# Snake convolutions: where the first three chunks of hats lie, and the order of the last 9x9 sums against the second chunk's hats

## The chip, the cores and the metric

One core of one Trainium2 chip runs the whole program. The metric is device time in microseconds, as a median of several runs; one further execution was profiled. In the profile, TensorE is PE (with PEld for its weight loads), VectorE is DVE, ScalarE is ACT, GpSimd is POOL, and SyncE is SP. SP does no arithmetic here: it issues the transfers (DMAs), one after the other in program order.

## The reference, cut to what matters

The program is four layers on an image x of 2 x 128 x 64 x 64: an attention layer, a snake-convolution layer (L1), three steps of two 3x3 convolutions, and a four-direction selective scan. The change is in L1, which computes

```python
h  = gelu(affine(conv2d(x, cv1_w, 1), cv1_g, cv1_b))             # 64 channels
o0 = silu(affine(conv2d(h, conv0_w, K // 2), conv0_g, conv0_b))  # 9x9
ox = dsconv(h, ..., morph=0)   # nine samples along a row, shifted by learnt offsets
oy = dsconv(h, ..., morph=1)   # the same along a column
out = silu(affine(conv2d(concatenate([o0, ox, oy]), fuse_w, 0), fuse_g, fuse_b))
```

In dsconv, a 3x3 convolution of h gives offsets, whose running sums from the centre tap give a position for each pixel and tap; h is sampled there with linear interpolation, the samples are multiplied with the weights w, and the result is group-normalised. Then the layer gates out and adds x.

## The kernel before, in words

`layer1` (L466 on) first calls `stem_and_wide`, then `snakes`. `stem_and_wide` computes the stem (h, kept as `hz`) and the 9x9. The 9x9 is done with a fast scheme: six combinations of the columns of h, `comb[0]` to `comb[5]`, are multiplied on TensorE with six transformed weights (`w`, L590), in the order x = 1, 2, 3, 4, 0, 5, once for each half k of the image. After each x, VectorE and ScalarE gather the products into the four sums s, p, d and q of each image b; a sum that is complete gets its silu on ScalarE (L658) and is put on the list `ready`. `fuse` (L598) multiplies a ready sum with its part of the fuse weights, and copies the product into the image `xa`, on VectorE for image 0 (L604) and on ScalarE for image 1 (L602). The jobs that x leaves on the list are fused after the products of the next x; so the two s of x = 0 are fused behind the products of x = 5, and the two q of x = 5 last.

The snakes sample by multiplication with hats. For each chunk of 4 lines (17 chunks for each of two directions, called chunk 0, 1, 2 and so on here), `positions` has SP load 1 MB of positions from the scratch `pos` in DRAM, broadcast to the partitions, by four transfers of 256 KB each (L794). `hat` turns them into interpolation weights in place: an absolute value on ScalarE (L802), then a subtraction and a minimum on VectorE (L803). `transposed` puts lines of h on the partitions (L784, copied by ScalarE in L785); `sample` multiplies lines with hats into PSUM (L859), copied to `feat` by ScalarE for image 0 (L873) and VectorE for image 1 (L871); `convolve` multiplies the samples with the weights of the taps (L885 and L896), once for every two chunks from the third on.

Class `Ahead` does some of this beside the last products of the 9x9 (second half, x = 0 and x = 5). `load` fetches the offset and tap weights; `convs` computes the offsets ahead of the products of x = 5; `beside` is called before each pair of those products: at n = 2 it writes the positions to `pos` and loads chunks 0 and 1 (`positions(0, m, near[m])`), at n = 12 and 15 it transposes lines, and at n = 24 it makes the hats of chunk 0. What it fills lies in the tile `early`, of pool l1big, which outlives the 9x9: `early` is a window of four combinations, `comb[1]` to `comb[4]`, whose space is filled anew once their products are done. `comb[0]` and `comb[5]` lie in the pool of the 9x9, l1a.

`snakes` opens its pools where l1a was. Chunks go round four slots: `near[0]` and `near[1]` in `early`, and `hats0` and `hats1`, allocated in `snakes`. So chunks 2 and 3 are loaded into space that the 9x9 has used until its end. The body of `snakes` first issues the load of chunk 2 and the hats of chunk 1 (`positions(0, 2)`, `hat(0, 1)`). Step n then loads chunk n + 3, transposes lines for n + 2, samples chunk n, makes the hats of chunk n + 2, and at even n from 2 on convolves.

[...] The build does not always keep the written order there: the hats of chunk 1, written in `snakes`, stand some places earlier. So the order is given as built. ScalarE's order at the end of the 9x9 is: L802 of chunk 0, L802 of chunk 1, L602 (s of image 1), L658 twice (q), L602 (q of image 1). VectorE's is: L803 of chunk 0, L803 of chunk 1, L604 (s of image 0), L655 twice (the adds that complete q), L604 (q of image 0).

Of the kernel before, what the change touches and what calls it, by code (L numbers as in the profile page):

```python
# [10 lines left out]
F32 = mybir.dt.float32  # L11
# [9 lines left out]
P = 128  # L21
NB = 2
HW = 64
# [7 lines left out]
KC = K9 // 2  # L31
# [434 lines left out]
def layer1(g, I):  # L466

    nc, tc = g.nc, g.tc
    with ExitStack() as ctx:
        big = ctx.enter_context(tc.tile_pool(name="l1big", bufs=1))
        hz = big.tile([P, H8, H8], F32, name="hz")
        fw = big.tile([P, 3, P], F32, name="fw")
        nc.scalar.dma_start(fw, I["fuseT"])
        early = big.tile([P, 4, 3, HW // 2 + KC, HW // 4], F32, name="early")
        dr = ctx.enter_context(tc.tile_pool(name="l1dr", bufs=1, space=bass.MemoryType.DRAM))  # L480
        pos = dr.tile([64, L], F32, name="pos")
        ahead = Ahead(g, I, hz, early, pos)
        stem_and_wide(g, I, hz, fw, early, ahead)
        with ExitStack() as bctx:
            snakes(g, bctx, hz, ahead, fw)


def stem_and_wide(g, I, hz, fw, early, ahead):
# [10 lines left out]
    NF = HW // 4  # L499
# [3 lines left out]
    with ExitStack() as ctx:  # L503
# [1 line left out]
        ps = ctx.enter_context(tc.tile_pool(name="l1ps", bufs=8, space=PSUM))  # L505

        spdq = [[a.tile([P, BLK], F32, name=f"{n}{b}") for n in "spdq"] for b in range(NB)]
        comb = [early[:, i - 1] if 0 < i < 5 else a.tile([P, NQ, CR, NF], F32, name=f"comb{i}") for i in range(NX)]

        cw = comb[5].rearrange("p q r i -> p (q r i)")[:, : 9 * 64].rearrange("p (t o) -> p t o", o=64)  # L510
        nc.sync.dma_start(cw, I["cv1T"])
# [83 lines left out]
        def fuse(k, b, c, t):  # L595

            pf = ps.tile([P, BLK], F32, name="m")
            nc.tensor.matmul(pf, fw[:, 0, :], t, start=True, stop=True)  # L598
            xv = interior(g, b, k * RP, RP)[:, :, c : c + 4 * NF - 3 : 4]
            src = pf.rearrange("p (r i) -> p r i", i=NF)  # L600
            if b:
                nc.scalar.copy(xv, src)  # L602
            else:
                nc.vector.tensor_copy(xv, src)  # L604

        with tc.manual_schedule():
            for k in range(NBLK):
                stem(k)
                if k < 3:
                    wide_weights(0, 3 * k)  # L610
                if k * RB < CR:
                    combine(0, 1, k * RB, min((k + 1) * RB, CR))
            for t0 in (3, 0, 6):
                wide_weights(1, t0)
            for x in (3, 0, 5):
                combine(0, x, 0, CR)
            ready = []
            for k in range(HW // RP):
                for x in (1, 2, 3, 4, 0, 5):
                    last = k == HW // RP - 1  # L620
                    if last and x == 0:
                        ahead.load(w)
                    if last and x == 5:
                        ahead.convs(ps)
                    m = [ps.tile([P, BLK], F32, name="m") for b in range(NB)]
                    for n, pair in enumerate(zip(*(product(m[b], x, b, k) for b in range(NB)))):
                        if last and x == 5:
                            ahead.beside(n, ps)
                        for f in pair:
                            f()  # L630
                    for job in ready:
                        fuse(*job)
                    ready = []
                    for b in range(NB):
                        s, p, d, q = spdq[b]
                        if x == 1:
                            nc.scalar.copy(s, m[b])
                        elif x == 3:
                            nc.scalar.copy(p, m[b])
                        elif x == 2:  # L640
                            nc.vector.tensor_sub(d, s, m[b])
                            nc.vector.tensor_add(s, s, m[b])
                        elif x == 4:
                            nc.vector.tensor_sub(q, p, m[b])
                            nc.vector.tensor_add(p, p, m[b])
                            stt(d, q, 2.0, d, ALU.mult, ALU.add)
                            stt(q, q, 6.0, d, ALU.mult, ALU.add)
                            nc.vector.tensor_add(s, s, p)
                            stt(p, p, 3.0, s, ALU.mult, ALU.add)
                            ready += [(k, b, 1, d), (k, b, 2, p)]  # L650
                        elif x == 0:
                            nc.vector.tensor_add(s, s, m[b])
                            ready.append((k, b, 0, s))
                        else:
                            nc.vector.tensor_add(q, q, m[b])  # L655
                            ready.append((k, b, 3, q))
                    for _, _, _, t in ready:
                        nc.scalar.activation(t, t, AF.Silu, bias=vec(g, "conv0_b"), scale=vec(g, "conv0_g"))  # L658
                    if k == 0 and x not in (1, 3):
                        combine(1, {2: 1, 4: 3}.get(x, x), HW - CR, HW)  # L660
            for job in ready:
                fuse(*job)


class Ahead:
# [6 lines left out]
    def __init__(self, g, I, hz, early, pos):  # L672

        self.g, self.I, self.hz, self.pos = g, I, hz, pos
        e = early.rearrange("p n q r i -> p (n q r i)")
        self.at = 0

        def take(n):
            self.at += n
            return e[:, self.at - n : self.at]  # L680

        self.dsc = take(2 * P).rearrange("p (d o) -> p d o", d=2)
        self.dsw = take(2 * KC * P).rearrange("p (d t o) -> p d t o", d=2, t=KC)
        self.grp = take(P)
        self.lines = take(self.SLOTS * self.CN * 64).rearrange("p (r i c) -> p r i c", r=self.SLOTS, i=self.CN)
        self.near = [self.as_hats(take(2 * self.NT * self.CN * HW)) for _ in range(2)]
        self.cmat = take(64)
        self.ov = take(3)
        self.ob = take(1)
        self.placed = None  # L690

    def as_hats(self, t):
# [2 lines left out]
    def load(self, w):  # L695

        g, I = self.g, self.I
        dma = g.nc.sync.dma_start
        c = w.rearrange("p y q x o -> p (y q) (x o)")[:, :, P : 5 * P]
        self.yt = c[:64, 0:NBLK]  # L700
        self.grid = c[:, 8:12]
        self.th = [c[:, 12], c[:, 13]]
        self.y0 = [c[:, 14], c[:, 15]]
        self.ow = [c[:, 16 + t // 8, t % 8 * 64 : t % 8 * 64 + 64] for t in range(9)]
        dma(c[:, 16].rearrange("p (t o) -> p t o", o=64), I["offT"][:, :8])
        dma(self.ow[8], I["offT"][:, 8])
        for e in range(2):
            half = slice(64 * e, 64 * e + 64)
            dma(self.ov[half], I["offv"])
            dma(self.cmat[half], I["cum"])  # L710
            dma(self.grid[half], I["grid"].rearrange("p (k e x) -> p k e x", e=2, x=BLK)[:, :, e, :])
        g.nc.vector.scalar_tensor_tensor(
            self.ob, self.ov[:, 0:1], self.ov[:, 1:2], self.ov[:, 2:3], ALU.mult, ALU.add
        )
        dma(self.grp, I["grp_div"])
        for b in range(2):
            half = slice(64 * b, 64 * b + 64)
            dma(self.dsc[half], I["dscT"][:, :, KC])
            dma(self.dsw[half], I["dscT"][:, :, b * (KC + 1) : b * (KC + 1) + KC])
# [41 lines left out]
    def beside(self, n, ps):  # L761

        if n == 2:
            self.place(*self.placed, ps)
            for di in range(2):
                rows = slice(32 * di, 32 * di + 32)
                self.g.nc.sync.dma_start(self.pos[rows].rearrange("p (c x) -> p c x", c=NBLK), self.yt[rows])
            for m in range(2):
                self.positions(0, m, self.near[m])
        elif n in (12, 15):  # L770
            self.transposed(0, (n - 12) // 3, ps.tile([P, BLK], F32, name="m"))
        elif n == 24:
            self.hat(self.near[0])
# [32 lines left out]
def snakes(g, ctx, hz, ahead, fw):  # L806
# [10 lines left out]
    psf = ctx.enter_context(tc.tile_pool(name="l1psf", bufs=4, space=PSUM))  # L817
    psa = ctx.enter_context(tc.tile_pool(name="l1psa", bufs=1, space=PSUM))

    far = [ahead.as_hats(bp.tile([P, 2 * NT * CN * HW], F32, name=f"hats{i}")) for i in range(2)]  # L820
    slots = ahead.near + far
    feat = bp.tile([P, NB, RING, NT, HW], F32, name="feat")
    oraw = bp.tile([P, NB, L], F32, name="oraw")
    hats = {}
# [8 lines left out]
    def positions(di, m):  # L833

        if di < 2:
            hats[di, m] = slots[(di * NCH + m) % len(slots)]
            ahead.positions(di, m, hats[di, m])
# [118 lines left out]
        return turns  # L956

    with tc.manual_schedule():
        for m in range(2):
            hats[0, m] = slots[m]  # L960
        positions(0, 2)
        hat(0, 1)
        for n in range(2 * NCH):
            di, m = divmod(n, NCH)
            if m == 0:
# [1054 lines left out]
```

## Time and profile before

| what | value |
|---|---|
| median of 3 runs | 5577.32 us (5575.88 to 5578.47) |
| the profiled execution | 5576.86 us, of which its span is 5574.9 us |
| busy share of the span: PE, DVE, ACT, POOL | 85%, 81%, 73%, 65% |
| 9x9 products (L590), first to last start | 1147.6 to 1466.2 us |
| snake samples from the hats of slots hats0 and hats1 (L859), first to last start | 1494.3 to 1741.4 us |
| load of positions, four per chunk (L794) | 136 transfers of 256 KB, median 9.8 us from issue to landing |

Times in the trace are microseconds from the start of the span. The profiled execution took 1.96 us more than its span (work around the first and last instruction), and is 0.46 us below the median; so a difference read in the span is carried to the median as it is. The row of a stretch gives the busy time of each engine in it, and PEclk, the TensorE clock that was granted, as a share of the full clock. In the chain, each line is a piece of the work that ended last, with what it is and on which engine; SPq is the issue of a transfer, and DMA is the time from the end of the issue to the landing.

### The profile page before, as it was taken

To read this page: it belongs to the slowest core of one execution; us is meant where nothing else is said; L and a number is where in the kernel's file an instruction comes from. 1 tells how busy PE (TensorE), PEld (TensorE's weight loads), DVE (VectorE), ACT (ScalarE), POOL (GpSimd) and SP (SyncE) were. 2 spreads that over 40 slices of the span, in tenths; PEclk is the share of its full clock that TensorE was granted. 3 is DMA by queue.
4 is the path that set the end of the run, shared out by engine and by line. 5 is a ranking of instruction groups with operands and counts; after the bars stand their busy time and mean duration, and the time that the engine had idled before them with its cause. 6 is when DMAs were issued, how large, how long until landed. Compare 5 with 4: busy or idle time off the path is not lost.

```text
span 5574.9 us, 54509 instructions
## 1 busy us (share of the span) xinstructions
PE 4717.5 (85%) x17062; PEld 1756.9 (32%) x17062; DVE 4540.1 (81%) x4240; ACT 4087.5 (73%) x6282; POOL 3642.2 (65%) x1189
## 2 busy tenths in 40 slices
PE   6999999899887799878888777777787888777886
PEld 3444444344443344222222222222222222222221
DVE  6565655562245997799999999999999999999998
ACT  3999999600255212798888888888888888888886
POOL 6222222100000311699999999999999999999999
PEclk8999999999999999888887888888888887888887
DMA  4111111300464000555556555655655565565554
GB/s 155 39 46 41 36 31 38 62 1 16 79 122 78 22 0 0 125 129 142 134 127 142 138 132 127 145 127 136 151 129 130 139 142 133 128 142 136 136 134 106
DMA packets 335161, 554.27 MB, mean 99 GB/s; under 512 B 69408, under 2 KB 116016, under 8 KB 334736
## 3 DMA queue, kind: packets, MB, share of 16 engines
q1 hardware_dynamic: 333456, 549.27, 41.7%
q8 instruction: 135, 2.21, 0.2%
q10 hardware_dynamic: 1408, 1.46, 0.1%
q14 instruction: 162, 1.33, 0.1%
HBM read 461.40 MB, written 89.13 MB: 99 GB/s over the span
## 4 chain that ended last, share of the span: by engine, by line
DVE 43%; PE 35%; ACT 10%; issue 6%; DMA 2%; POOL 2%; SPq 1%; DVEq 0%; POOLq 0%; ACTq 0%
DVE db L1607 29%; DVE db L1571 10%; PE ps L312 8%; PE acc L328 8%; PE m L1161 6%; PE m L590 4%; ACT da L1593 4%; PE acd L896 2%; ACT db L1599 1%; DVE gt L1634 1%; PE m L550 1%; ACT L1458 1%; ACT u L1458 1%; PE pf L859 1%; POOL db L1617 1%
## 5 line engine op out<-in xcount | busy, mean ns | idle before, releaser
L1617 POOL TENSOR_TENSOR db<-db,c 128x2048 f32<-128x2048 f32 x512 | 2312.7, 4532 | 47.4 <-ACT hl L1612 33.0
L1593 ACT ACTIVATE da<-dd,am 128x512 f32<-128x512 f32 x2048 | 1398.3, 687 | 300.3 <-DVE db L1607 279.7
L1607 DVE TENSOR_TENSOR_SCAN db<-da,db 128x512 f32<-128x512 f32 x1376 | 1584.9, 1203 | 35.2 <-ACT db L1599 28.2
L318 ACT ACTIVATE e<-ps 128x1536 f16<-128x1536 f32 (+1 forms) x683 | 919.0, 1624 | 8.0 <-PE ps L312 8.0
L1607 DVE TENSOR_TENSOR_SCAN db<-da,hl,db 128x512 f32<-128x512 f32 x672 | 825.8, 1271 | 40.8 <-POOL db L1580 3.4
L1571 DVE TENSOR_TENSOR db<-pbc,dd 128x2048 f32<-128x2048 f32 (+1 forms) x384 | 780.7, 2033 | 31.5 <-PE pbc L1550 31.5
L1580 POOL TENSOR_TENSOR db<-b,dd 128x2048 f32<-128x2048 f32 (+1 forms) x192 | 772.7, 4025 | 13.8 <-DMA b<-bx 13.8
L1625 PE MATMUL py<-db,fold 128*32 128x512 f32 x4096 | 602.7, 674 | 153.9 <-POOL db L1617 153.7
L312 PE MATMUL ps<-q 128*128 128x512 f16 x2048 | 554.0, 379 | 4.3 <-DVE flag L260 2.7
L328 PE MATMUL acc<-e,v 128*128 128x512 f16 x2048 | 553.6, 379 | 0.1
L346 POOL TENSOR_TENSOR parts<-parts 32x512 f32<-32x512 f32 x64 | 80.5, 1257 | 707.8 <-DVE parts L345 707.8
L1599 ACT ACTIVATE db<-da,db,hl 128x1 f32<-128x1 f32 x1120 | 393.9, 352 | 148.7 <-DVE db L1571 103.6
L1212 POOL MEMSET v<- 128x256 f32 x2 | 1.1, 554 | 711.9 <-DVE b L1050 711.9
L339 DVE RECIPROCAL rec<-acc 32x512 f32<-32x512 f32 x64 | 214.9, 3358 | 257.8 <-PE acc L328 248.3
L1161 PE MATMUL m<-v,u 128*128 128x512 f32 x864 | 378.0, 600 | 43.1 <-DVE v L1104 41.5
L1518 PE MATMUL pm<-dd,ident 128*128 128x512 f32 x512 | 357.4, 836 | 2.9 <-ACT dd L1511 2.7
L1477 PE MATMUL pm<-u,wxp 128*72 128x512 f32 x256 | 186.4, 870 | 141.4 <-ACT u L1458 141.4
L1550 PE MATMUL pbc<-bc,sel 64*128 64x512 f32 x384 | 207.1, 539 | 109.2 <-DVE db L1571 108.4
L312 PEld LDWEIGHTS <-q 128*128 128x128 f16 x2048 | 197.7, 97 | 278.4 <-issue 103.8
L328 PEld LDWEIGHTS <-v 128*128 128x128 bf16 x2048 | 199.2, 97 | 248.9 <-issue 10.2
L1625 PEld LDWEIGHTS py<-db,fold 128*32 128x32 f32 x4096 | 90.0, 113 | 551.5 <-issue 326.0
L1453 PE MATMUL pm<-xn,wcs 128*128 128x512 f32 x512 | 235.3, 603 | 17.0 <-ACT xa L1652 10.5
(332 smaller groups left out, 6614.6 us busy)
## 6 DMA issues: line engine op xcount, KB each, us to landing
dd<-dx SPq DMA_DIRECT2D x1024, 256.0 KB, 6.4
dx<-dd SPq DMA_DIRECT2D x128, 512.0 KB, 5.5
c<-bx SPq DMA_DIRECT2D x1024, 64.0 KB, 2.1
b<-bx SPq DMA_DIRECT2D x512, 64.0 KB, 4.6
early<-pos SPq DMA_DIRECT2D x72, 256.0 KB, 9.8
piece<-qd SPq DMA_DIRECT2D x128, 128.0 KB, 2.8
hats<-pos SPq DMA_DIRECT2D x64, 256.0 KB, 9.7
piece<-kd SPq DMA_DIRECT2D x112, 128.0 KB, 2.7
```

What stands on the lines that cost most here:

```text
L312: nc.tensor.matmul(ps[:, i, :], t[:, 1, kb * P : (kb + 1) * P], t[:, 0, qb * BLK : (qb + 1) * BLK], start=True, stop=True,)
L318: nc.scalar.activation(e[:, :n, :], ps[:, :n, :], AF.Exp, scale=1.0 / UP**2)
L328: nc.tensor.matmul(acc, v3[b][:, kb, h, :], e[:, i, :], start=(kb == 0), stop=(kb == NS - 1))
L1161: nc.tensor.matmul(m[x], weights[j][:, dy, x, :], v[j][b][:, x, r0 : r0 + RP, :].rearrange("p r i -> p (r i)"), start=(dy == 0), stop=(dy ...
L1518: nc.tensor.matmul(ps, g.ident, S[i]["dd", hf][:, x, :], start=(x == 0), stop=(x == 1))
L1571: nc.vector.tensor_tensor(db_tile(k)[:, :, :n], G[k].pop("pb")[:, :n].unsqueeze(1).to_broadcast([P, 4, n]), S[i]["d4", hf][:, 1, :, :n], A ...
L1580: nc.gpsimd.tensor_tensor(db_tile(k)[:, :, n:], S[i]["b", ng][:, n:].unsqueeze(1).to_broadcast([P, 4, BLK - n]), S[i]["d4", hf][:, 1, :, n ...
L1593: nc.scalar.activation(da, S[i]["d4", hf][:, 0, q, :], AF.Exp, scale=am[:, hf, q, ng : ng + 1])
L1599: nc.scalar.activation(b0, da[:, first : first + 1], AF.Identity, bias=b0, scale=hl[:, hf, ng, q, :])
L1607: nc.vector.tensor_tensor_scan(d1, d0, d1, 0.0 if zero else hl[:, hf, ng, q, :], ALU.mult, ALU.add)
L1617: nc.gpsimd.tensor_mul(v, v, S[i]["c", ng].unsqueeze(1).to_broadcast([P, 4, BLK]))
L1625: nc.tensor.matmul(S[i]["y", hf][32 * q : 32 * q + 32, :], fold, G[k]["db"][:, q, :], start=False, stop=(ng == NNG - 1),)
```

## The change

`early` becomes a window of five combinations, `comb[0]` to `comb[4]`, and only `comb[5]` stays in l1a. The larger window holds three chunks of hats, `near[0]` to `near[2]`, now at its start, followed by the tap weights and the lines; three small constants (`cmat`, `ov`, `ob`) move to an unused corner of the 9x9's weights. `beside` loads three chunks at n = 2 instead of two, and `snakes` allocates one slot, `hats3`, instead of two. After the products of the last x = 5, the two s are not fused first: q is completed and gets its silu, then all four sums are fused. `hat` of chunk 1 is called at the end of `stem_and_wide` and no longer in `snakes`.

```diff
-        early = big.tile([P, 4, 3, HW // 2 + KC, HW // 4], F32, name="early")
+        early = big.tile([P, 5, 3, HW // 2 + KC, HW // 4], F32, name="early")
...
-        comb = [early[:, i - 1] if 0 < i < 5 else a.tile([P, NQ, CR, NF], F32, name=f"comb{i}") for i in range(NX)]
+        comb = [early[:, i] for i in range(5)] + [a.tile([P, NQ, CR, NF], F32, name="comb5")]
...
-                    for job in ready:
-                        fuse(*job)
-                    ready = []
+                    ended = last and x == 5
+                    if not ended:
+                        for job in ready:
+                            fuse(*job)
+                        ready = []
...
-                    for _, _, _, t in ready:
+                    for _, _, _, t in ready[2 * ended :]:
                         nc.scalar.activation(t, t, AF.Silu, bias=vec(g, "conv0_b"), scale=vec(g, "conv0_g"))
...
             for job in ready:
                 fuse(*job)
+            ahead.hat(ahead.near[1])
...
+        self.near = [self.as_hats(take(2 * self.NT * self.CN * HW)) for _ in range(3)]
         self.dsc = take(2 * P).rearrange("p (d o) -> p d o", d=2)
...
-        self.near = [self.as_hats(take(2 * self.NT * self.CN * HW)) for _ in range(2)]
-        self.cmat = take(64)
-        self.ov = take(3)
-        self.ob = take(1)
...
+        self.cmat, self.ov, self.ob = c[:, 17, 64:128], c[:, 17, 128:131], c[:, 17, 131:132]
...
-            for m in range(2):
+            for m in range(3):
                 self.positions(0, m, self.near[m])
...
-    far = [ahead.as_hats(bp.tile([P, 2 * NT * CN * HW], F32, name=f"hats{i}")) for i in range(2)]
-    slots = ahead.near + far
+    slots = ahead.near + [ahead.as_hats(bp.tile([P, 2 * NT * CN * HW], F32, name="hats3"))]
...
-        for m in range(2):
+        for m in range(3):
             hats[0, m] = slots[m]
-        positions(0, 2)
-        hat(0, 1)
```

In the built program the number of instructions of each engine and their order elsewhere are the same as before. ScalarE's order at the end of the 9x9 becomes: absolute value of chunk 0, silu of q twice, the two copies, absolute value of chunk 1. VectorE's becomes: minimum of chunk 0, the two adds of q, the two copies, the first two copies of samples, minimum of chunk 1.

## The prediction

> **What bounds the kernel now.** I read the page first: PE 85%, DVE 81%, ACT 73% of the span, which says nothing of one stage. The change lies around 1450 to 1500 us, so I asked for stretches there.
>
> ```profile
> core 0: us, PE busy (x) PEld busy (x) DVE busy (x) ACT busy (x) POOL busy (x), PEclk, DMA share, GB/s
> 1466.00:1468.60 2.60, 2.60 (x8) 0.68 (x4) 0.78 (x1) 0.02 (x1) 0.00 (x0) 1.00 0.21 50
> 1468.60:1474.20 5.60, 0.01 (x1) 0.00 (x0) 3.31 (x4) 3.80 (x4) 0.00 (x0) 0.94 0.00 0
> 1474.20:1479.10 4.90, 3.78 (x4) 1.18 (x4) 1.07 (x1) 1.74 (x2) 0.00 (x0) 0.50 0.00 0
> 1479.10:1486.30 7.20, 7.12 (x112) 6.49 (x112) 1.11 (x4) 1.37 (x6) 0.00 (x0) 0.68 0.77 90
> 1486.30:1494.30 8.00, 0.00 (x0) 0.00 (x0) 1.26 (x2) 3.23 (x4) 0.00 (x0) 0.77 0.86 179
> 1494.30:1501.10 6.80, 6.56 (x38) 3.41 (x38) 1.88 (x3) 2.75 (x4) 0.00 (x0) 0.77 0.79 154
> 1501.10:1598.00 96.90, 96.85 (x804) 55.89 (x808) 42.77 (x56) 52.43 (x66) 0.00 (x0) 1.00 0.80 148
> ```
>
> PE is without a gap in the 9x9 and again from 1501.1 to 1598. Between them it stands still twice (5.6 and 8.0 us), no bytes move for 10 us, and it works at a half clock after each halt. The chain of waits names the cause:
>
> ```profile
> 1459.24 9.23 DMA early<-pos
> ...
> 1468.58 2.01 ACT early L802
> ...
> 1470.61 1.23 DVE early L803
> 1471.84 0.97 DVE xa L604
> 1472.81 0.53 DVE q L655
> ...
> 1473.36 0.82 ACT q L658
> ...
> 1474.23 3.80 PE m L598 x4
> ...
> 1478.04 0.57 SPq L794
> ...
> 1487.15 11.10 DMA hats<-pos
> ...
> 1498.35 2.00 ACT hats L802
> ```
>
> So the last sums of the 9x9 stand in ACT's and DVE's queues behind the hats of chunk 1, whose positions land at 1468.5; only when those sums are fused (1478.0) may SP load chunks 2 and 3 into their space; and the landing of chunk 3 (1498.25) sets when PE goes on. SP's own wait has one line:
>
> ```profile
> SPq L794 <- PE m L598: 16.3, 1, 16.3
> ```
>
> **The order at the end of the 9x9.** After the change, ACT and DVE do the hats of chunk 0 first, as now: DVE ends them at 1465.55 + 1.23 = 1466.78. The products of x = 5 end at 1466.6. Then come the adds of q, 2 x 0.67 us, from 1466.8 to 1468.1 (they start at 1472.65 now). Now 1.58 us pass from the first add's start to PE's fuse (1472.65 to 1474.23), so q can be fused from 1468.4; the two s occupy PE from 1466.63 to 1468.61 and hide that. The fuse of q follows at once: 1.98 us as that of s took at full clock, in place of 3.80 at half. It ends at 1470.6, not 1478.0. ACT's last copy (L602, 1.06 us) ends at 1471.7, and PE starts the snakes at 1471.8, not 1479.16: 7.35 us earlier. Chunk 1's absolute value comes only after that copy (1471.7 to 1473.7), its minimum on DVE behind two small copies of samples (0.42 us) to about 1475.5. Queued behind it are the copies of chunk 0's samples, and PE's samples of chunk 1; before those PE has two transposes and the samples of chunk 0 to do (four microseconds at full clock), until 1475.9. So that moved piece costs nothing; if PE were faster, at most 0.5 us.
>
> **The load of chunk 2, moved.** Four transfers of SP go right behind chunk 1's eighth, from 1461.6 (1450.07 + 11.56), where SP has nothing to do until 1478. Nothing else is in SP's queue behind them but chunk 3's load. Their space, combinations 2 and 3, has been read for the last time when x = 3 ends; chunk 0 now lies on combination 0, whose products end at 1402, chunk 1 on combinations 1 and 2. No wait for the 9x9 is left on any of them.
>
> When does it land? ACT's first touch of each chunk shows the landings, since it waited for the DMA: 1463.52 (chunk 0), 1468.58 (1), 1491.01 (2), 1498.35 (3), 1506.03 (4), 1513.34 (5). With further chunks queued behind, one takes (1513.34 - 1491.01) / 3 = 7.44 us; with nothing behind, chunk 1 took 5.06. So chunk 2 lands between 1473.6 (5.06 behind chunk 1) and 1478.4 (1463.5 + 2 x 7.44); I take 1478, near the full queue, since the queue is now full. The earlier load may also slow chunk 1 to at most 1463.5 + 7.4 = 1470.9, which is before ACT reads it (1471.7).
>
> **The load of chunk 3.** Its slot lies where q of image 1 was, so it waits for the last fuse, 1470.6 instead of the present 1478.0 (SP issued it at 1480.6, behind chunk 2). Its landing from both sides: 1468.58 + 2 x 5.06 = 1478.7 at the fastest spacing; 1463.5 + 3 x 7.44 = 1485.8 at the full queue's. A third way: chunk 2 took 13.0 us from its first issue to ACT (1478.04 to 1491.01), which gives 1483.6. I take 1484.5, between the last two, nearer the row that the queue will be like. That is 13.85 us before 1498.35.
>
> **When PE goes on.** Now PE resumes the convolution at 1501.15, which is 2.80 us after ACT starts on chunk 3: ACT does the absolute value (2.00), a copy, and then the copies of chunk 2's samples, for which PE waits. After: 1484.5 + 2.8 = 1487.3. The other condition is PE's own work after chunk 2: absolute value 2.0, minimum 1.2, samples about 2.2, the first products of the convolution 2.1 + 1.1, with gaps some 9 us: 1478 + 9 = 1487. Both meet at 1487.3. Even with earlier landings PE can't be there before about 1484.4 (1475.5 for chunk 1's hats, then its samples, ACT's copies of them, and chunk 2's hats and samples).
>
> **The clock.** The Trainium skill, "TensorE: Matmul & The Clock Gate", Part 1, says that the clock halves after a wholly idle window of about 3.4 us, windows running freely, and comes back after as long a busy one. The row first: 5.6 and 8.0 us idle both led to 0.50, and the four matmuls behind the first took 3.8 us for 2.0. After the change one gap is left, from chunk 1's samples (1479) to chunk 2's hats (about 1481.5), 2.5 to 3 us. By the rule it is too short, and the sum stands. By the trace alone, which has no gap of that length at full clock, it could count as those did; then samples and first products (5.3 us) take twice as long, and the saving falls to about 9 us. The gap lies close to the limit that the rule gives, so this speaks against the change; I take the rule, since no idle window of its length fits in.
>
> **The rest costs nothing.** The three small constants move, and `load` makes the same eleven transfers; they are issued by 1387, and the constants are first needed when the running sums of the first offsets start at 1421.4. Chunk 4 may be issued once chunk 0 is sampled (1475) and SP has issued chunk 3 (about 1475), so the stream stays full. From then on PE binds (96.85 of 96.9 us) and everything is shifted, the two later layers too; nothing there runs to a time of its own.
>
> Sum: 1501.15 - 1487.3 = 13.9 us. The span goes from 5574.9 to 5561.0, the profiled time from 5576.86 to 5563.0; that execution was 0.46 below the median, so the median goes from 5577.3 to 5563.4.
>
> **The rivals.**
>
> - *The transfers are the bound.* If the stream keeps 7.44 us a chunk from chunk 0 on, chunk 5 is there at 1463.5 + 5 x 7.44 = 1500.7, 12.6 us earlier than 1513.34, and chunk 7 at 1515.6 against 1527.79, 12.2 earlier. PE has little cover (ACT waited for chunks 4, 5 and 7), so the saving shrinks to 12, or to 10 if the added transfers also delay chunk 0, for whose hats DVE's adds of q must wait: 5565.3 to 5567.3. For it: the DMA share of 0.8 throughout. Against it: 181 GB/s and more in single stretches.
> - *The clock halves in the new gap:* 9 us saved, 5568.3.
> - *Chunk 2 isn't early in effect* (some wait keeps it back until the last fuse at 1470.6): then only the order gains, 7.35 us, 5570.0.
> - *Chunks land at the fastest spacing:* PE's own limit, 1501.15 - 1484.4 = 16.7 us, 5560.6.
> - *Slower.* PE's granted clock falls in the stretch from 1487 to 1584, which is 96.9 us at full clock with PE never idle. At a mean clock f it costs 96.9 x (1/f - 1): the gain of 13.9 is gone at f = 0.875, and below f = 0.794 (25.1 us) the kernel is slower by over 0.2%; at 0.75 it costs 32.3, which gives 5577.3 + 18.4 = 5595.7. For it: the mean over the whole span is 0.883. Against it: 1.00 in this and in every stretch of the 9x9 without idle time, so the low values come with idleness.
>
> **How the numbers follow.** The forecast has 0.62, the slow transfers 0.20, the half clock 0.06, only the order 0.05, the fastest spacing 0.03, slower 0.04. The predicted time is 5563.4. Its own bounds, chunk 3 at 1485.8 or PE's limit, give 12.3 to 16.7 us: 5560.6 to 5565.0. For 8 in 10 I add the slow transfers, up to 5567.5, and a little below for a faster tail: 5559.5 to 5568.0. A measurement tells 0.2% from no change, 11.2 us, so 5566.2: faster holds the forecast, the fastest and two thirds of the slow transfers, 0.78; same holds the rest of these, the half clock and the order, 0.18; slower 0.04.
>
> **What the profile after would show.** The fuse of q (L598) ends near 1470.6 with four matmuls in 2 us; the snakes' first transpose near 1471.8; SP issues twelve transfers from 1450 in one run; ACT starts on chunk 2 near 1478 and on chunk 3 near 1484.5; PE runs without a gap from about 1487; PEclk stays 1.00. Wrong would be: ACT on chunk 3 past 1486, PE waiting for hats after 1490, PEclk 0.50 between 1475 and 1490, or chunk 0's hats later than 1463.5.

## The result, and the profile after

The changed kernel takes 5567.54 us (median of 21 runs, 5565.31 to 5571.33) against 5576.42 us before in as many runs: the ratio is 0.9985, with a 95% interval of 0.9978 to 0.9991. Two further comparisons gave 0.9985 (0.9977 to 0.9992) and 0.9984 (0.9976 to 0.9992). The kernel is faster by some 9 us, where 13.9 us were forecast; the time lies near the upper end of the range, and the change is a little under the 0.2% that were given as the bound of "faster".

The stretches of the profile after, cut at the same events as the stretches of before (the columns are those named in the prediction):

```profile
1468.50:1472.20 3.70, 3.65 (x10) 1.32 (x8) 3.22 (x5) 2.49 (x4) 0.00 (x0) 1.00 0.83 146
1472.20:1479.60 7.40, 6.13 (x112) 5.79 (x112) 2.36 (x6) 3.99 (x7) 0.00 (x0) 1.00 0.84 149
1479.60:1483.20 3.60, 0.01 (x1) 0.03 (x1) 1.32 (x2) 3.24 (x4) 0.00 (x0) 0.85 0.69 151
1483.20:1490.00 6.80, 6.80 (x37) 3.56 (x38) 1.10 (x2) 1.60 (x1) 0.00 (x0) 0.58 0.77 144
1490.00:1491.20 1.20, 0.61 (x3) 0.00 (x1) 0.77 (x1) 1.20 (x4) 0.00 (x0) 1.00 0.53 99
1491.20:1588.00 96.80, 96.80 (x810) 55.54 (x811) 43.79 (x56) 53.08 (x67) 0.00 (x0) 1.00 0.80 147
```

The halt of 5.6 us at the end of the 9x9 and the stretch without any transfer are gone. Of the two halts one is left, 3.6 us ahead of the samples of chunk 2, and the clock halves behind it (0.58 in that stretch). The products of the 9x9 end at 1468.5 here and at 1466.6 before, so times are compared from there. ACT's own timeline shows chunks 1 to 4:

```profile
1473.05 2.00 ACT L803 ACTIVATE early<-early,vecs 128x2048 f32<-128x2048 f32 x1
1479.84 2.00 ACT L803 ACTIVATE early<-early,vecs 128x2048 f32<-128x2048 f32 x1 [3.58 <-issue]
1488.40 2.00 ACT L803 ACTIVATE hats<-hats,vecs 128x2048 f32<-128x2048 f32 x1 [5.32 <-DMA hats<-pos]
1495.04 2.00 ACT L803 ACTIVATE early<-early,vecs 128x2048 f32<-128x2048 f32 x1 [3.41 <-issue]
```

Chunk 2 is there 11.3 us after the end of the products (24.3 before), chunk 3 after 19.9 us (31.7 before), and ACT, with nothing else ahead of it, waits 5.32 us for its landing (the positions of chunk 3 lie in `hats`). The chain of waits runs accordingly:

```profile
1468.52 3.65 PE m L598 x8
...
1472.19 1.07 ACT xa L602
...
1473.30 1.04 PE pb L785 x13
...
1483.36 7.31 DMA early<-pos
1490.67 0.49 ACT feat L873
...
1491.20 6.28 PE acd L896 x14
```

The eight matmuls of the last fuse are one run of 3.65 us at full clock, as forecast; behind them come the start of the snakes, up to 1479.6, and then nothing but transfers before the convolution's resumption at 1491.20. The chain names a load into `early` there, chunk 4's; that it is chunk 3's landing that counts is read from ACT's own row above, since the copy L873 that PE waits for stands in ACT's queue behind the absolute value of chunk 3.

Three profiles of each kernel (two more of each are among the runs below) divide the whole program as follows. Each row is the difference of two times in the trace, in us.

| part | before | after | mean difference |
|---|---|---|---|
| start to the first product of the 9x9 | 1147.6, 1146.8, 1146.6 | 1149.4, 1148.5, 1150.1 | +2.3 |
| products of the 9x9 | 319.1 each | 319.1 each | 0.0 |
| end of the products to the first statistics (L908) | 148.6, 149.5, 150.2 | 136.8, 136.2, 136.5 | -12.9 |
| first to second statistics | 147.9, 150.7, 150.2 | 148.6, 150.8, 148.7 | -0.3 |
| second statistics to the first scan | 514.3, 514.9, 513.6 | 514.4, 516.4, 514.2 | +0.7 |
| first scan to the end | 3297.4, 3297.0, 3296.8 | 3298.4, 3298.1, 3298.3 | +1.2 |

The rows add up to -9.0 us, close to the measured difference of 8.9. In the stage of the change 12.9 us are gained; 4.2 us are lost in parts whose instructions are the same in both kernels. The time at half clock does not explain that loss. Ahead of the 9x9 it is 61.4 us in all six profiles; from the first scan on it is 1136.6, 1085.4 and 1199.6 us before, and 1129.8, 1153.7 and 1146.9 after.

Where it lies can be read from the starts of VectorE's instructions in the six traces. Of the 2.3 us ahead of the 9x9, 1.9 are there by 170 us, in the part that begins with the landing of the inputs; over the next 890 us the six profiles keep their distances to within 0.1 us. The 0.7 us before the first scan is no more than the spread of one kernel. From the first scan on it is not the instructions that take longer: VectorE is busy for 3208.0, 3207.2 and 3206.8 us before, and for 3208.0, 3206.9 and 3206.8 us after. What has grown is its idle time, from 89.4, 89.8 and 90.0 us to 90.4, 91.3 and 91.4. One such place, in the kernel before and then in the changed one:

```profile
4864.18 2.26 DVE L1571 TENSOR_TENSOR db<-pbc,dd 128x2048 f32<-128x2048 f32 x1
4866.55 2.46 DVE L1607 TENSOR_TENSOR_SCAN db<-da,hl,db 128x512 f32<-128x512 f32 x2
```

```profile
4854.88 2.27 DVE L1569 TENSOR_TENSOR db<-pbc,dd 128x2048 f32<-128x2048 f32 x1
4857.61 2.46 DVE L1605 TENSOR_TENSOR_SCAN db<-da,hl,db 128x512 f32<-128x512 f32 x2 [0.46 <-ACT hl L1610]
```

The two instructions are as long in both; the pause between them is 0.11 us in all three profiles of before, and 0.46 us in all three of after. Why it differs is open.

### The profile page after: what moved, and what is told of

It reads as the page before. It is cut to its first block, busy times and chain, and to the rows that moved or that the text cites. A ratio compares the mean times of both kernels' runs of the same rounds, so it can differ in the third digit from the quotient of the medians.

```text
span 5566.7 us, 54515 instructions
## 1 busy us (share of the span) xinstructions
PE 4707.2 (85%) x17062; PEld 1751.6 (31%) x17062; DVE 4541.1 (82%) x4240; ACT 4087.1 (73%) x6282; POOL 3641.8 (65%) x1189
## 4 chain that ended last, share of the span: by engine, by line
DVE 45%; PE 36%; ACT 10%; issue 5%; DMA 2%; POOL 1%; SPq 0%; DVEq 0%; POOLq 0%; ACTq 0%
DVE db L1605 30%; DVE db L1569 10%; PE ps L312 8%; PE acc L328 8%; PE m L1159 6%; PE m L590 5%; ACT da L1591 3%; PE acd L896 2%; DVE gt L1632 1%; ACT db L1597 1%; PE m L550 1%; PE pf L859 1%; ACT L1456 1%; ACT u L1456 1%; PE pm L1475 1%
## 5 line engine op out<-in xcount | busy, mean ns | idle before, releaser
L1578 POOL TENSOR_TENSOR db<-b,dd 128x2048 f32<-128x2048 f32 (+1 forms) x192 | 772.8, 4025 | 12.8 <-DMA b<-bx 12.8
L1451 PE MATMUL pm<-xn,wcs 128*128 128x512 f32 x512 | 234.0, 600 | 19.9 <-ACT xa L1650 10.8
```

Of the source, the lines that this page charges most:

```text
L1578: nc.gpsimd.tensor_tensor(db_tile(k)[:, :, n:], S[i]["b", ng][:, n:].unsqueeze(1).to_broadcast([P, 4, BLK - n]), S[i]["d4", hf][:, 1, :, n ...
```

## The experiments

All positions below are microseconds from the end of the 9x9's last product in the profile of each run. The convolution resumes with its third matmul of L896, the first that needs ACT's copies of chunk 2's samples, which ACT makes behind the absolute value of chunk 3.

| run | q fused | ACT starts chunk 2 | chunk 3 | convolution resumes | first statistics | median of the kernel (before, beside it) |
|---|---|---|---|---|---|---|
| before (3) | 11.2 to 11.7 | 24.3 to 24.7 | 31.7 to 32.0 | 34.5 to 34.9 | 148.6 to 150.2 | |
| after (3) | 3.6 to 4.0 | 11.3 to 12.3 | 19.2 to 19.9 | 22.1 to 22.9 | 136.2 to 136.8 | 5567.5 (5576.4) |
| only the order | 3.6 | 16.7 | 24.1 | 26.9 | 140.9 | 5570.1 (5576.9) |
| only the space | 13.8 | 17.8 | 26.9 | 29.8 | 146.2 | 5575.4 (5576.9) |
| offsets earlier | 3.6 | 7.6 | 16.9 | 19.7 | 136.5 | 5571.3 (5576.9) |
| clock kept up | 3.7 | 11.4 | 20.1 | 22.9 | 139.6 | 5569.4 (5580.8) |
| half of chunk 3 | 3.7 | 10.7 | 13.8 | 20.6 | 135.3 | one run, 5565.4 (5580.8) |
| both of these | 3.8 | 10.8 | 13.9 | 19.6 | 134.7 | one run, 5567.4 (5580.8) |
| pieces of 4 KB | 4.0 | 8.0 | 12.4 | 16.7 | 128.6 | 5557.3 (5579.2) |

The kernel before lies between 5576.4 and 5580.8 us in these comparisons, so a time is read against the one beside it. Each run but before and after has a single profile, and the first statistics of one kernel lie up to 1.6 us apart between profiles.

**The changed kernel again,** to see where its time goes in a second execution.

> The changed kernel once more, for the time of its parts in a second execution. Theory: the saving lies between the end of the 9x9 and the convolution's resumption (11.8 us in the two profiles), and the 1.9 us by which the 9x9 ended later in the first profile of the changed kernel are chance: here the products of x = 5 end within 1 us of 1466.6, or at another time that is as often earlier as later; time 5567 to 5568. Rival: the new layout of memory costs time ahead of the 9x9: they end at 1468.5 again.

Measured: 5569.36 us, ratio 0.9985. The first statistics come after 136.2 us, so the gain in the stage repeats. The products of the 9x9 end at 1467.6, between the two values named. A third time:

> The changed kernel a third time, for the interval of its ratio and one more profile. Theory (12 us gained up to the statistics of the first direction, nothing systematic after that): that stretch again 136 to 137 us against 149, the whole kernel 8 to 12 us faster than before. Rival (a later part gives back 3 us): the whole kernel 9 us or less, and the parts behind the first direction longer than in both profiles of before by 2 us or more.

Measured: 5569.61 us beside 5579.15 us, ratio 0.9984; the stage takes 136.5 us. The products end at 1469.3, and the part from the first scan on is again 3298.3. So neither of the two clear outcomes came true: the stage is 12.9 us shorter, and yet 3 to 4 us are lost elsewhere, half of them ahead of the stage, not behind it.

**The kernel before again,** twice.

> The kernel before once more, for the length of its parts: up to the 9x9, from the end of its products to the statistics of the first direction (148.6 us in the first profile), from there to those of the second (147.9), and the rest. Theory (what the change gains up to the first statistics, 12 us, is kept, and the difference to the measured 9 is chance in the first profile): the second direction is as long as in the changed kernel's two profiles (148.6 and 150.8), within 1.5 us. Rival (the second direction or a later part gives 2 to 3 us back): 148 again, so shorter than in all the others.

> The kernel before against itself, in as many rounds: how far two medians of one kernel lie apart (1 to 3 us expected), and a third profile of the length of its parts: about 149 us from the end of the 9x9's products to the first statistics.

Measured: the second direction takes 150.7 and 150.2 us, so the 147.9 of the first profile were short by chance, and the change gives nothing back there that can be told. Against itself the kernel before had a ratio of 1.0003 (0.9994 to 1.0011). The time at half clock between the two statistics is 22.1 us in the profile with 147.9 and 28.4 in that with 150.7, but 23.6 in the one with 150.2, so the clock is at most a part of this spread.

**Only the order** of the last sums, with two chunks early:

```diff
+                    ended = last and x == 5
+                    if not ended:
+                        for job in ready:
+                            fuse(*job)
+                        ready = []
...
+                    for _, _, _, t in ready[2 * ended :]:
...
+            ahead.hat(ahead.near[1])
...
-        hat(0, 1)
```

> The memory as before (two chunks early), only the order of the last sums and of chunk 1's hats as in the changed kernel. Theory (a stream of transfers at its own pace): the 9x9's end comes 7.5 us earlier, chunks 2 and 3 are issued then and land as long after that as before (20.2 us after the first issue), so the convolution resumes 7.5 us earlier and the kernel is 7 to 8 us faster than before, about 5569. Rival (the early load is what pays, the order is hidden behind the hats of chunk 3): within 2 us of before.

Measured: ratio 0.9987 (0.9980 to 0.9994), 6.8 us between the medians; the convolution resumes 7.7 us earlier than before. The order alone brings most of the gain. In the same comparison the changed kernel takes 5569.36 us against 5570.09 here, which is no clear difference; that the space adds to the order is seen in the stage alone, 136.5 us against 140.9.

**Only the space,** with three chunks early and the order of before (the hats of chunk 1 in `snakes`, the two s fused first):

> Three chunks early as in the changed kernel, but the order at the end of the 9x9 as before. Theory: chunk 1 lands about 2.5 us later since more is queued, and the last sums wait for its hats, so the 9x9 ends 2 to 3 us later than before; chunk 3 is issued then and needs some 13 us, so it is ready some 4 to 5 us earlier than before: 5571 to 5573. Rival (the early load alone brings the whole gain): 5567 to 5568.

Measured: ratio 0.9997 (0.9988 to 1.0005), no difference that can be told. The chain of waits of this run:

```profile
1458.76 11.61 DMA early<-pos
...
1470.47 2.01 ACT early L800
...
1476.12 3.75 PE m L598 x4
...
1481.83 11.06 DMA hats<-pos
```

Four more transfers behind it make chunk 1 come some 2.3 us later (4.4 us after the products, where it was 1.9 to 2.2), and with the order of before the last sums wait for its hats: the fuse of q ends 13.8 us after the products instead of 11.3, and chunk 3 is issued that much later. The convolution resumes only 4.9 us earlier. There the two parts nearly add up: together they give 12.1 us, where 7.7 + 4.9 are 12.6.

**The offsets earlier,** to start the stream of loads sooner:

```diff
-                    if last and x == 5:
-                        ahead.convs(ps)
...
+                        if last and x == 0 and n == 18:
+                            ahead.convs(ps)
...
-        if n == 2:
+        if n == 0:
```

> The changed kernel with the convolutions of the offsets placed amid the products of x = 0 and the loads at the start of those of x = 5, so chunks 0 to 2 are issued some 10 us earlier against the end of the 9x9, and chunk 3 meets an empty queue. If the stream's pace from chunk 0 on sets when chunk 3 lands (theory), chunk 3 lands some 3 us earlier and the kernel gains 3 to 6 us on the changed one: 5562 to 5565. Rival (chunk 3's own latency from its issue at the end of the 9x9 sets it, however empty the queue): no more than 1 us.

Measured: ratio 0.9991 (0.9984 to 0.9997), 2.0 us behind the changed kernel in the same comparison, though the intervals of the two ratios overlap. The edit did not do what it was to do. The last offsets are still placed at the start of x = 5, so the loads start only 1.7 us earlier against the end of the products, and PE now waits for a tanh there:

```profile
PE m L742 <- ACT w L738: 3.2, 1, 3.2
```

Those 3.2 us lengthen the 9x9. Chunk 3 is there 2.7 us earlier and the convolution resumes at 19.7, 2.8 us earlier; but the first statistics still come after 136.5 us. Two things eat the gain. PE's wait behind chunk 3 is 3.13 us long here, and the clock is at half for 3.4 us behind it, where the changed kernel is at full clock again: that takes 1.7 us. The rest goes at the change of direction, where PE comes to its next halt 1.3 us earlier and waits 1.1 us longer. The chain of the changed kernel shows what ends that halt:

```profile
1590.88 11.14 DMA hats<-pos
...
1602.13 2.01 ACT hats L803
...
1604.17 1.23 DVE hats L804
1605.39 0.52 DVE mv L908 x2
```

The first statistics stand on VectorE behind hats of the second direction, and these wait for a load. It lands 133.5 us after the products in the changed kernel and 133.3 us here, so what PE gains before that is lost in the wait.

**The clock kept up.** Three matmuls are put into the gap before chunk 2's samples; their product is not used:

```diff
             transposed(*divmod(n + 2, NCH))
+            if n == 2:
+                spare = psa.tile([P, RB, HW], F32, name="acd0")
+                for _ in range(3):
+                    nc.tensor.matmul(spare, fw[:, 0, :], hz[:, KC : KC + RB, KC : KC + HW], start=True, stop=True)
```

> The changed kernel with three matmuls more on PE (3 us at full clock), their product unused, put between the transposes and the samples of chunk 2, where PE stood still and its clock then halved. Theory (chunk 3's landing sets when the convolution resumes): the clock stays at 1.00, and the convolution still resumes 22 to 23 us after the end of the 9x9's products, time as the changed kernel's. Rival (the halved clock sets it): 2 to 4 us earlier there and in the time.

Measured: the convolution resumes 22.9 us after the products, no earlier. PE's timeline of the changed kernel first, and then of this run:

```profile
1483.20 4.24 PE L859 MATMUL pf<-early 64*64 64x256 f32 x32 [3.60 <-ACT feat L873]
1487.37 2.18 PE L885 MATMUL acd<-hz,early 64*128 64x512 f32 x4
1489.48 1.12 PE L896 MATMUL acd<-feat,early 128*128 128x512 f32 x2
1491.20 1.98 PE L896 MATMUL acd<-feat,early 128*128 128x512 f32 x4 [0.59 <-ACT feat L873]
```

```profile
1477.62 2.84 PE L970 MATMUL acd<-hz,fw 128*128 128x512 f32 x6
1481.34 2.50 PE L859 MATMUL pf<-early 64*64 64x256 f32 x32 [0.88 <-ACT feat L873]
1483.77 2.08 PE L885 MATMUL acd<-hz,early 64*128 64x512 f32 x4
1485.78 1.12 PE L896 MATMUL acd<-feat,early 128*128 128x512 f32 x2
1489.49 2.98 PE L896 MATMUL acd<-feat,early 128*128 128x512 f32 x4 [2.58 <-ACT feat L873]
```

At full clock the samples take 2.50 us instead of 4.24, and PE waits 2.58 us behind chunk 3 instead of 0.59: what the clock gives, the wait takes. The wait of 2.58 us then halves the clock in its turn, from 1490.3 to 1493.8, so the first statistics come 3 us later than in the changed kernel. The ratio is 0.9979, and its interval (0.9971 to 0.9987) overlaps that of the changed kernel. In the other two profiles of the changed kernel PE does not wait at this place at all; this is the third one:

```profile
1491.18 7.13 PE L896 MATMUL acd<-feat,early 128*128 128x512 f32 x16
```

So there PE's own work at half clock ends when the copies are there: two bounds meet within 0.6 us, and taking away the half clock alone leaves chunk 3's.

**Half of chunk 3,** without and with these matmuls:

```diff
+        if nx == 1:
+            self.g.nc.gpsimd.memset(hats[:, 1], 0.0)
         for b in range(NB):
-            for x in range(2):
+            for x in range(nx):
```

Here nx is 1 for chunk 3 of the first direction, and else 2. The kernel leaves out half of that chunk's positions, so its samples there are wrong; only its times are used.

> The changed kernel with only half of chunk 3 loaded (two transfers of four; the other half of its hats' positions is set to zero on POOL, so the samples of chunk 3 are wrong in that part). Theory: chunk 3 is ready some 4 us earlier; the convolution then resumes only about 1 us earlier, since PE's own work after chunk 2, at half clock, ends only then. Rival (chunk 3 alone sets it): 3 to 4 us earlier. If the stream of transfers counts for what follows, chunks 4 and 5 are earlier by about 3.7 us too.

> Both together: half of chunk 3, and the three matmuls that keep the clock up. Theory (two bounds that nearly meet, chunk 3 and the half clock): only both together let the convolution resume 3 to 4 us earlier than in the changed kernel, at about 19 us after the end of the 9x9's products, as it was forecast at 20.7. Rival: no earlier than with half of chunk 3 alone.

Measured: chunk 3 is there 5.8 us earlier, and PE then has no wait for it. With half of chunk 3 alone the convolution goes on at 20.6, 1.9 us earlier; with the matmuls too, at 19.6. So chunk 3 held the resumption back, and the halved clock is worth 1.0 us more, but only once chunk 3 is out of the way. That half of chunk 3 brought more than the 1 us expected goes back to the clock: the gap before chunk 2's samples was 2.88 us here, and the clock stayed at half for 3.4 us (1482.1 to 1485.5), not 6.8 as in the changed kernel. And the first statistics come only 1.2 and 1.8 us earlier than in the changed kernel.

**Pieces of 4 KB.** A chunk is 1 MB in 1024 pieces of 1 KB, since the rows of four taps lie apart in DRAM. Here they are copied once more in DRAM, in the order of the chunks:

```diff
+        packed = dr.tile([8, HW // Ahead.CN - 1, Ahead.NT * Ahead.CN * HW], F32, name="packed")
...
-            for m in range(3):
-                self.positions(0, m, self.near[m])
+            self.positions(0, 0, self.near[0], False)
+            self.pack(0, self.g.nc.scalar)
+            for m in range(1, 3):
+                self.positions(0, m, self.near[m])
+            self.pack(1, self.g.nc.sync)
...
+                eng.dma_start(
+                    self.packed[4 * di + 2 * b + x].rearrange("m (t y) -> m t y", t=self.NT),
+                    self.source(di, b, x, 0, n).rearrange("t (m y) -> m t y", m=n),
+                )
...
+                    self.g.nc.sync.dma_start(
+                        hats[64 * b : 64 * b + 64, x].rearrange("p t i h -> p (t i h)"),
+                        self.packed[4 * di + 2 * b + x, m].partition_broadcast(64),
+                    )
```

> The changed kernel with the positions copied once more in DRAM, in the order of the chunks (eight copies of 240 KB), so chunks 1 to 14 of each direction are loaded in pieces of 4 KB instead of 1 KB; the number of bytes of a load is the same. Theory (the pace of the stream of loads, 7.5 us a chunk in pieces of 1 KB, sets when the convolution resumes): a chunk takes 4 to 5 us, chunk 3 is ready 3 us or more earlier, the convolution resumes at PE's own limit, 17 to 19 us after the 9x9's products instead of 22.6, and waits at the change of direction shrink: 5 to 10 us faster than the changed kernel. Rival (the bytes written set the pace, whatever the pieces): 7 us a chunk as now, time as the changed kernel's or some us worse by the copies.

Measured: 5557.27 us, ratio 0.9964 (0.9950 to 0.9977) to the kernel before, and faster than the changed kernel as well. The transfers between 1500 and 1590 us (all packets, then count, size and median time from issue to landing of the loads), of the changed kernel and then of this run:

```profile
DMA packets 13715, 13.33 MB, mean 148 GB/s; under 512 B 807, under 2 KB 13706, under 8 KB 13706
early<-pos SPq DMA_DIRECT2D x37, 256.0 KB, 9.6
hats<-pos SPq DMA_DIRECT2D x15, 256.0 KB, 9.6
```

```profile
DMA packets 5585, 13.36 MB, mean 148 GB/s; under 512 B 807, under 2 KB 2855, under 8 KB 5578
early<-packed SPq DMA_DIRECT2D x32, 256.0 KB, 6.5
hats<-packed SPq DMA_DIRECT2D x8, 256.0 KB, 5.2
```

The same bytes land in 5 to 6.5 us instead of 9.6. In that stretch the loads here at times pause, and a shorter queue shortens a landing too. So the pace is better read where loads stand in line in both kernels, in this stretch of the changed kernel and then of this run (the last column is GB/s):

```profile
1476.00:1480.00 4.00, 3.43 (x56) 3.19 (x54) 1.13 (x3) 0.41 (x2) 0.00 (x0) 1.00 0.84 145
1476.00:1480.00 4.00, 4.00 (x66) 3.35 (x62) 2.58 (x4) 2.81 (x5) 0.00 (x0) 1.00 1.03 229
```

Chunk 3 is there 12.4 us after the products, the convolution resumes at 16.7, and the first statistics come 7.9 us earlier still than in the changed kernel.

## Why the prediction was right or wrong

Two terms of the sum failed. The landing of chunk 3 was put at 17.9 us after the products and came at 19.2 to 19.9, so the resumption gained 12.1 us and not 13.9. And all that comes outside the stage was put at nothing ("The rest costs nothing", "everything is shifted"), where it cost 4.2 us; the cause of that cost stays open. With 0.8 us more that were gained up to the first statistics, and 0.3 up to the second, some 9 us are left. The mechanism inside the stage, the order and the earlier load, was right.

**The order at the end of the 9x9: right.** Forecast were 1.98 us for the fuse of q at full clock and a snake stage that starts 7.35 us earlier. It starts 4.8 to 5.1 us after the products instead of 12.4 to 12.8, so 7.7 us earlier.

**Chunk 2, moved: right.** ACT was forecast to start on it at 1478, which is 11.4 us after the products; it was 11.3 to 12.3. No wait for the 9x9 was left on its load. Chunk 1, delayed by the queue, did not hold ACT up: ACT came to it 4.5 to 5.1 us after the products without idle time before it, as the prediction had it.

**The load of chunk 3: the term that was too small.** 1484.5 was taken, 17.9 us after the products, as a value between 13.0 us from its issue and the pace of the full queue. Measured are 19.2 to 19.9. The full queue's pace holds from chunk 0 on: chunk 0 came 3.1 us before the end of the products, so (19.9 + 3.1) / 3 = 7.7 us a chunk in the first profile, and 7.4 and 7.5 in the others, against the 7.44 of the row. That row's answer, 1485.8 or 19.2 us, would have been right. The 13.0 us that pulled the estimate down were those of a load into an empty queue; when chunk 3 was issued, 3.7 us after the products, all of chunk 2 and the end of chunk 1 were still under way. So the convolution resumes some 12 us earlier, not 13.9. This is the rival "the transfers are the bound", with its forecast of 12 us for the stage; that half of chunk 3 and the pieces of 4 KB both bring the resumption forward shows its cause. The halved clock is a second bound, within 0.6 us of it.

**The clock: wrong, with no effect on the time that a run shows.** The gap was forecast at 2.5 to 3 us, too short for the rule as it was used there (a wholly idle window of about 3.4 us); it was 3.6 us (3.7 and 4.2 in the other profiles), and the clock was 0.50 from 1482.1 to 1488.9. The longer gap is not the whole reason. The clock's changes stand 3.41 us apart or a multiple of it (it was at half for 6.83 us here, for 3.41 with half of chunk 3), and in the 3.41 us that ended at 1482.1 PE was busy for 0.9 us. With half of chunk 3 a gap of 2.88 us halved the clock, and with the added matmuls one of 2.58 us, with some 0.9 us of work in the 3.41 us before the change each time; in the third profile of the changed kernel it was 1.65 us. So here windows with up to 1.65 us of work sufficed, and the measurement decides against the rule of the Trainium skill, "TensorE: Matmul & The Clock Gate", Part 1, as the prediction read it. The choice that the trace alone left open, that the gap counts, was the right one. But at the resumption it left 12 us and not 9, since chunk 3 was as late and hid it. That the whole kernel gained 9 us, the figure of this rival, is chance: it comes from the losses outside the stage.

**"From then on PE binds and everything is shifted": right in its number for the stage, wrong for the whole.** The gain of some 12 us at the resumption is 12.9 at the first statistics. But it is not PE that binds up to there: at the change of direction PE waits for a load, and the 2.8 us that the earlier offsets gained before it were lost in it. The shift held because that load moved by 11.9 us as well (133.5 us after the products, 145.4 before). And the parts with the same instructions cost 4.2 us more: 2.3 before the 9x9, 0.7 and 1.2 in the later layers. The sum took such parts for fixed. In all thirteen profiles, the part up to the 9x9 takes 1146.4 to 1150.1 us, and the part from the first scan on 3296.8 to 3299.6, where one program repeats itself within 1.7 and 0.6. Five programs that share the changed kernel's layout ahead of the 9x9 have 1146.4, 1146.9, 1147.4, 1147.6 and 1149.3, so the layout isn't the cause; the order-only program, with the memory of before, has 1148.9. The loss arises at the start of the program and in the pauses between the instructions of the scan, as shown above. What makes these differ stays open; no run separated it. It makes 4 us of a forecast of 14 uncertain in a program of 5570 us, and the sum had no term for it. That the time still fell inside the range owes something to its width: the range was widened for slow transfers.

The chances put 0.78 on faster by over 0.2%; it was 0.15%, a size that the prediction gave to the half clock alone or the order alone. It came from neither.

## What to carry to other kernels

Here a load that was moved forward into a queue that was then never empty landed at the queue's pace, counted from the first transfer on. So count chunks times the pace of the full queue, and leave the latency of a single load aside. If that pace is the bound, change the pieces: the same bytes in 4 KB instead of 1 KB were worth more here than the whole reordering. And before a gain of a few microseconds is carried from a stage to a long program, see by how much parts with equal instructions differ in length from program to program.

## What the runs showed of the hardware that was not expected

PE's clock halved after gaps of 2.6 to 3.1 us, in which no window of 3.41 us was wholly idle, and stayed full over those of 1.2 us. Parts with the same instructions took lengths that differ between programs and repeat within one: from the first scan to the end 3297.4, 3297.0 and 3296.8 us in the kernel before, and 3298.4, 3298.1 and 3298.3 in the changed one. VectorE was busy for the same time in both; its pauses differed, at the place shown 0.11 us in one program and 0.46 in the other. And transfers of 256 KB that are broadcast to 64 partitions ran at 145 GB/s in pieces of 1 KB and at 229 GB/s in pieces of 4 KB in the stretches shown, with loads in line in both.
